# A graph network kernel: slot numbers by one comparing and multiplying operation, lists of 120 edges, the count moved to ScalarE

## The chip, the cores and the metric

The kernel runs on one core of a Trainium2 chip. The core has five engines with queues of their own: TensorE (PE: matrix products, with weight loads shown as PEld), VectorE (DVE), ScalarE (ACT), GpSimd (POOL) and SyncE (SP, which here only issues DMAs). Each engine works through its queue in order and waits on semaphores for the others. The metric is the device time of one execution in microseconds; the median of three runs is what is compared.

## What is computed

The reference takes 6250 nodes with 64 features and 206,250 edges (100,000 drawn pairs in both directions, and a loop at every node), sorted by destination. Cut to what matters:

```python
edge_index = jnp.stack([src, dst])
h = relu(layernorm(x))
# GIN layer, twice: agg = segment_sum(h[src], dst); mlp2(h + agg)
x = x + L0(h, edge_index)
h = relu(layernorm(x))
# message layer: y = mlp3(h[src]); z = segment_sum(y, dst); mlp3([h, z])
x = x + L1(h, edge_index)
```

All three sums over edges use the same 6250 x 6250 matrix of edge counts, A. The kernel builds A from the edge lists once, as one-byte numbers, and then makes matrix products with it.

## The kernel before

**Stages.** Nodes are padded to 49 tiles of 128. From the start to about 375 us the function `fast` builds A tile by tile and takes the first sum over edges from each freshly built tile, with the first layers' products mixed in. Then two sweeps read A back from DRAM for the second and third sum (line 761). A check at the end of the building sets `bad`; where it is set, the slow function `general` computes everything again. It isn't set for these inputs.

**How a tile of A is made.** Two neighbouring destination nodes make a pair, and 128 pairs (one on each partition) make a pair tile; there are 25, one for every two tiles of A. For each pair tile:

- `search` (line 304) and `search_block` (line 328) find where each pair's edges begin, by Sign activations on ScalarE, first over 375 samples and then over a block of 550 gathered destinations.
- `fetch_edges` (line 339) turns that into offsets on VectorE (`off_f`, `off`, lines 344 and 345) and issues one indirect DMA on GpSimd for each pair tile and list: 128 consecutive entries of `dst` into `d_win` and of `src` into `s_win`, for every pair (line 349). `fetch_blocks` (line 319) gathers the blocks for a later batch in the same way (line 324).
- `slots` (line 355) makes three numbers for every entry on VectorE: `word` (which of 32 words), the `high` part of the source (which of 49 columns of tiles), and a `place` number that says which byte of the word and which node of the pair is meant. The windows can hold edges of other pairs. So `mine` (line 376) compares each entry's pair with the partition's own (`which`) and counts the hits in `number`; line 380 then adds -64 to `high` for entries that hit. The one-hot pattern `high2` starts at `HB` = -64, so only those match.
- `cast` (line 392) copies `word` to 16 bits on ScalarE, `turn` (line 396) transposes the three numbers on TensorE, and ScalarE copies them to `lkw` (line 404).
- `hot` (line 406) makes one-hot matrices `there`, `high` and `low` on VectorE, from double-buffered tiles; `build` (line 434) multiplies them for 16 pairs at a time into the PSUM tile `cnt` (line 445; there are two such tiles), and ScalarE evicts each into the tile `a` (line 447). `store` (line 425) sends `a` to DRAM.

**Batches and order.** Pair tiles go in batches of one and then two (`BATCHES`), so that a batch is four tiles of A. The dictionary `beside` (line 523) says between which quarter tiles the steps for later batches are issued: `slots`, `cast` and `turn` one batch ahead, gathers three to four ahead. `follow` and `behind` give the scheduler an order on one engine; otherwise the scheduler places instructions by itself. `FirstSum.quarter` (line 584) puts the first-sum products of the tile before (line 588) between the counts of this one.

**The opening.** Before the rhythm is steady, seven blocks of seven tiles each are normalized (`values`, line 511: `norm` with VectorE steps, a Square and a square root on ScalarE) and each is split into three 16-bit parts (`split`, line 251: products on lines 258 and 260 into `cnt` tiles, copies on lines 255 and 261). Blocks 5 and 6 are issued after tile 0's counts (lines 620 and 624), with `search_block` and `search` for later batches between.

**The check.** `number` has one column per pair tile. Line 652 sums it, lines 656 and 657 count the columns over `SLOTS` = 120, and lines 659 to 668 compare the sums over all partitions with the number of edges, with the summed first-sum counts, and with 0.

Of the kernel before, what the change touches and what calls it, by code (L numbers as in the profile page):

```python
# [32 lines left out]
FP = mybir.dt.float32  # L33
I32 = mybir.dt.int32
I16 = mybir.dt.int16
BF = mybir.dt.bfloat16
# [3 lines left out]
AF = mybir.ActivationFunctionType  # L40
OP = mybir.AluOpType
AX = mybir.AxisListType

P = 128
N = 6250
E = 206250
# [11 lines left out]
H = NT  # L58
G = P // 2
NQ = (NT + 1) // 2  # L60
# [4 lines left out]
BATCHES = (1,) + (2,) * 12  # L65
MOST = max(BATCHES)
SLOTS = 120
# [1 line left out]
W = P // 4  # L69

ONE_BITS, SECOND_BIT, PLACE_BIT = (127 + 2) << 7, 2 + 7, 3 + 7
HB = -64
FIRST_HOTS = ((0, 16), (16, 16), (32, 32))
MIXED = (NT - 8) // 4 + 1
XT = 7
# [83 lines left out]
def fast(ctx: ExitStack, tc: tile.TileContext, x, src, dst, w, bad, out):  # L159

    nc = tc.nc
    dram = ctx.enter_context(tc.tile_pool(name="f_dram", bufs=1, space=bass.MemoryType.DRAM))
    const = ctx.enter_context(tc.tile_pool(name="f_const", bufs=1))
# [10 lines left out]
    def bank(name, dtype=FP):  # L174
        return pmix.tile([P, CH * 4 // mybir.dt.size(dtype)], dtype, tag="mix", name=name)
# [24 lines left out]
    high2 = once.tile([P, H, 2], BF, name="high2")  # L200
    nc.gpsimd.iota(high2, pattern=[[1, H], [0, 2]], base=HB, channel_multiplier=0, allow_small_or_imprecise_dtypes=True)
    which = once.tile([P, NQ], FP, name="which")
    nc.gpsimd.iota(which, pattern=[[P, NQ]], base=0, channel_multiplier=1, allow_small_or_imprecise_dtypes=True)
    ones = const.tile([P, P], FP, name="ones")
    nc.vector.memset(ones, 1.0)
    parts2 = [once.tile([P, MOST, 3, P], BF, name=f"parts{i}") for i in range(2)]


    smp_f = once.tile([SP_ROWS, SP_COLS], FP, name="smp_f")
# [6 lines left out]
    ps = bank("ps_smp")  # L216
# [11 lines left out]
    base = once.tile([P, NQ], FP, name="base")  # L228
    off_f = once.tile([P, NQ], FP, name="off_f")
    off = once.tile([P, NQ], I32, name="off")  # L230
    number = const.tile([P, NQ], FP, name="number")
    sums = const.tile([P, NT], FP, name="sums")

    def norm(to, t, n):
# [42 lines left out]
    wins = building.enter_context(tc.tile_pool(name="f_wins", bufs=2))  # L277
    hots = building.enter_context(tc.tile_pool(name="f_hots", bufs=2))
    starts = [sum(BATCHES[:b]) for b in range(len(BATCHES))]
    blks, lists, lkws = {}, {}, {}  # L280

    def tiles_of(b):
        return range(starts[b], starts[b] + BATCHES[b]), slice(starts[b], starts[b] + BATCHES[b])
# [3 lines left out]
    def behind(op, other):  # L287

        tc.add_manual_dep(op.ins, other.ins.name,
                          mybir.DependencyInfo(mybir.DependencyClass.NoSync, mybir.DependencyReason.DATA),  # L290
                          reason="order on an engine")
        return op

    def follow(op, engine):

        if engine in counted:
            behind(op, counted[engine])
# [30 lines left out]
    def search_block(b, i):  # L328

        if b >= len(BATCHES):  # L330
            return
        q = starts[b] + i
        blk = blks.pop(q)
        junk2 = wins.tile([P, BLK], BF, name="junk2", bufs=1)
        op = nc.scalar.activation(junk2, blk, AF.Sign, bias=below_node[:, q:q + 1], accum_out=sign2[:, q:q + 1])  # L335
        follow(op, "ACT")
        return op

    def fetch_edges(b):

        if b >= len(BATCHES):
            return
        each, qs = tiles_of(b)
        nc.vector.scalar_tensor_tensor(off_f[:, qs], sign2[:, qs], -0.5, base[:, qs], op0=OP.mult, op1=OP.add)
        nc.vector.tensor_scalar(off[:, qs], off_f[:, qs], float(E - P), None, op0=OP.min)  # L345
        lists[b] = [wins.tile([P, MOST, P], I32, name=name)[:, :len(each), :] for name in ("d_win", "s_win")]
        for win, of in zip(lists[b], (dst, src)):
            for i, q in enumerate(each):
                nc.gpsimd.indirect_dma_start(  # L349
                    out=win[:, i, :], out_offset=None, in_=of.rearrange("(a o) -> a o", o=1),  # L350
                    in_offset=bass.IndirectOffsetOnAxis(ap=off[:, q:q + 1], axis=0))

    words = {}

    def slots(b):

        if b >= len(BATCHES):
            return
        each, qs = tiles_of(b)
        n = len(each)  # L360
        d, s = lists.pop(b)

        def temp(name, dtype=I32, tag=None):
            return wins.tile([P, MOST, P], dtype, name=name, tag=tag or name, bufs=1)[:, :n, :]

        parts = parts2[b % 2][:, :n]

        def first(op):
            follow(op, "DVE")

        pair = temp("pair")
        first(nc.vector.tensor_scalar(pair, d, 1, PITCH // 2 - 1, op0=OP.logical_shift_right, op1=OP.bitwise_and))
        pair = pair.bitcast(I16).rearrange("p q (a b) -> p q a b", b=2)
        mine = temp("mine", FP)
        for i, q in enumerate(each):
            nc.vector.tensor_scalar(mine[:, i, :], pair[:, i, :, 0], which[:, q:q + 1], None,
                                    op0=OP.is_equal, op1=OP.add, accum_out=number[:, q:q + 1])
        high = temp("high_i")
        first(nc.vector.tensor_scalar(high, s, 7, 63, op0=OP.logical_shift_right, op1=OP.bitwise_and))
        nc.vector.scalar_tensor_tensor(parts[:, :, 1, :], mine, float(HB), high, op0=OP.mult, op1=OP.add)  # L380
        word = temp("word")
        first(nc.vector.tensor_scalar(word, s, 2, W - 1, op0=OP.logical_shift_right, op1=OP.bitwise_and))
        place = temp("place", tag="high_i")
        first(nc.vector.tensor_scalar(place, s, 3, PLACE_BIT, op0=OP.bitwise_and, op1=OP.logical_shift_left))
        second = temp("second", tag="mine")
        first(nc.vector.tensor_scalar(second, d, 1, SECOND_BIT, op0=OP.bitwise_and, op1=OP.logical_shift_left))
        place, second = (t.bitcast(I16).rearrange("p q (a b) -> p q a b", b=2)[:, :, :, 0] for t in (place, second))
        nc.vector.scalar_tensor_tensor(parts[:, :, 2, :].bitcast(I16), place, ONE_BITS, second,
                                       op0=OP.bitwise_or, op1=OP.bitwise_or)
        words[b] = word  # L390

    def cast(b):
        if b < len(BATCHES):
            follow(nc.scalar.copy(parts2[b % 2][:, :BATCHES[b], 0, :], words.pop(b)), "ACT")

    def turn(b, i):

# [126 lines left out]
    for b in range(len(BATCHES)):  # L524
        step = BATCHES[b]

        def at(u, what, *args):
            beside.setdefault(8 * starts[b] + u * step // 2, []).append((what, args))

        at(0, slots, b + 1)  # L530
        at(4, cast, b + 1)
        for i in range(BATCHES[b + 1] if b + 1 < len(BATCHES) else 0):
            at(7 + 2 * i, turn, b + 1, i)
        if b > 0:
            at(6, search, b + 4)
# [17 lines left out]
    values(0)  # L553
    search_block(0, 0)
    fetch_edges(0)
    values(XT)
    slots(0)
    cast(0)
    for i in range(2):
        op = search_block(1, i)  # L560
    fetch_edges(1)
    turn(0, 0)
    values(2 * XT)
# [84 lines left out]
    hz = late.tile([P, ROWS], FP, name="hz")  # L648


    stats = const.tile([P, 3], FP, name="stats")
    nc.vector.tensor_reduce(stats[:, 0:1], number, axis=AX.X, op=OP.add)
    nc.vector.tensor_reduce(stats[:, 1:2], sums, axis=AX.X, op=OP.add)
    nc.vector.tensor_scalar(stats[:, 1:2], stats[:, 1:2], UNIT, None, op0=OP.mult)
    over = const.tile([P, NQ], FP, name="over")
    nc.vector.tensor_scalar(over, number, float(SLOTS), None, op0=OP.is_gt)
    nc.vector.tensor_reduce(stats[:, 2:3], over, axis=AX.X, op=OP.add)
    ps = bank("ps_stats")
    nc.tensor.matmul(ps[0:1, 0:3], ones[:, 0:1], stats, start=True, stop=True)
    want = const.tile([1, 3], FP, name="want")  # L660
    nc.vector.memset(want[:, 0:1], float(E))
    nc.vector.memset(want[:, 1:2], float(E + ROWS))
    nc.vector.memset(want[:, 2:3], 0.0)
    good = const.tile([1, 3], FP, name="good")
    nc.vector.tensor_tensor(good, ps[0:1, 0:3], want, op=OP.is_equal)
    n_good = const.tile([1, 1], FP, name="n_good")
    nc.vector.tensor_reduce(n_good, good, axis=AX.X, op=OP.add)
    nc.vector.tensor_scalar(bad, n_good, 2.5, None, op0=OP.is_lt)


    follow(nc.vector.tensor_tensor(xs, xs, w.r4[:, None, :].to_broadcast([P, NT, D]), op=OP.add), "DVE")
# [114 lines left out]
    t, n = GROUPS[-1]  # L786
# [257 lines left out]
```

## Time and profile before

| what | value |
|---|---|
| median of three runs | 892.75 us (892.65 to 893.2) |
| the profiled execution | 895.53 us |
| its span, first to last instruction | 893.7 us |
| mean granted TensorE clock | 0.989 |
| TensorE busy | 854.5 us (96%) |
| VectorE busy | 633.7 us (71%) |
| ScalarE busy | 566.0 us (63%) |
| GpSimd busy | 126.9 us (14%) |
| DMA | 148,326 packets, 133.57 MB |

The profile comes from one execution. Busy time is the time in which an engine had an instruction at work; it does not say that the engine set the time. What did is read from the waits: a wait names the engine that the waiting one needed last. In a group's line stand source line, engine, operation, written and read tiles with their shapes, the count, total busy time and mean nanoseconds of one, and then the idle time just before them and who ended it. A timeline's line has the start and the duration first. In a line of a stretch of time, the number after an engine's busy time is its count of instructions, and the last three are the granted TensorE clock, the DMA engines' share and GB/s.

### The profile page before, as it was taken

What the parts mean: (1) busy time and instruction counts of PE and PEld (TensorE: products, weight loads), DVE (VectorE), ACT (ScalarE), POOL (GpSimd) and SP (SyncE); (2) the same over time, 40 slices, a digit from 0 to 9 for tenths busy, and PEclk for the clock granted to TensorE, in tenths of its full rate; (3) what the DMA queues carried; (4) which work ended last, traced back from release to release, by engine and by line L of the source; (5) the groups of instructions that cost most, each with busy time, mean ns of one, the idle gap of its engine ahead of it and who ended that gap; (6) DMA issues with size and microseconds to landing.
All of it is one profiled execution on the core that took longest, in us unless ns stands there. A gap on an engine that the chain in (4) does not pass through costs nothing.

```text
span 893.7 us, 19691 instructions
## 1 busy us (share of the span) xinstructions
PE 854.5 (96%) x8227; PEld 730.8 (82%) x8227; DVE 633.7 (71%) x908; ACT 566.0 (63%) x761; POOL 126.9 (14%) x86
## 2 busy tenths in 40 slices
PE   3789999999999999999999999999999999999996
PEld 1369999999999999978887878888889877777784
DVE  6889999999999999645545555554556676767662
ACT  5757776667776666645555555555546579777763
POOL 4535334354342200000000000000000000000000
PEclk9799999999999999999999999999999999999998
DMA  6335564455545534644444444444434677777771
GB/s 145 103 99 163 150 171 130 140 165 159 142 134 145 148 111 130 198 131 125 129 123 118 124 129 124 118 121 133 128 92 125 181 222 244 232 235 234 218 220 38
DMA packets 148326, 133.57 MB, mean 149 GB/s; under 512 B 29988, under 2 KB 110500, under 8 KB 148228
## 3 DMA queue, kind: packets, MB, share of 16 engines
q1 hardware_dynamic: 141784, 121.19, 46.5%
q0 software_dynamic: 3600, 10.32, 4.4%
q8 instruction: 66, 1.08, 0.5%
q10 hardware_dynamic: 2844, 0.72, 0.4%
q14 instruction: 32, 0.26, 0.1%
HBM read 91.25 MB, written 40.94 MB: 148 GB/s over the span
## 4 chain that ended last, share of the span: by engine, by line
PE 88%; ACT 4%; DMA 3%; DVE 2%; issue 2%; SPq 0%; POOL 0%; ACTq 0%; DVEq 0%
PE acc L761 43%; PE acc L588 23%; PE cnt L445 9%; PE ps_t L458 6%; PE ps_y L467 3%; ACT ar L754 2%; DMA a<-A 2%; PE ps_g L508 1%; PE cnt L258 1%; DMA xs<-in_x_dram 1%; ACT t L460 1%; ACT a L447 1%; PE acc L590 0%; DMA blk<-in_dst_dram,row 0%; PE ps_win L402 0%
## 5 line engine op out<-in xcount | busy, mean ns | idle before, releaser
L754 DVE CAST ar<-a 128x2048 fp32r<-128x2048 uint8 (+1 forms) x200 | 220.4, 1110 | 183.1 <-PE acc L761 158.4
L754 ACT CAST ar<-a 128x2048 fp32r<-128x2048 uint8 (+2 forms) x126 | 232.2, 1845 | 126.4 <-PE acc L761 108.6
L761 PE MATMUL acc<-ar,h2r 128*128 128x512 f32 (+2 forms) x1274 | 297.6, 388 | 0.0
L761 PEld LDWEIGHTS acc<-ar,h2r 128*128 128x128 f32 x1274 | 229.3, 188 | 49.8 <-issue 5.8
L588 PE MATMUL acc<-hp,a 128*128 128x193 bf16 x2401 | 237.1, 247 | 6.6 <-issue 5.8
L447 ACT ACTIVATE a<-cnt 128x784 int16<-128x784 f32 x196 | 160.8, 822 | 83.9 <-PE cnt L445 82.8
L588 PEld LDWEIGHTS <-a 128*128 128x128 fp8e4 x2401 | 196.4, 98 | 10.0 <-issue 7.8
L761 PE MATMUL acc<-ar,yr 128*128 128x512 f32 (+2 forms) x637 | 157.6, 399 | 0.0
L761 PEld LDWEIGHTS acc<-ar,yr 128*128 128x128 f32 x637 | 115.7, 188 | 32.5 <-issue 9.8
L445 PEld LDWEIGHTS <-low 128*128 128x128 fp8e4 x3136 | 107.6, 96 | 10.7 <-issue 10.4
L445 PE MATMUL cnt<-high,low 128*128 128x49 bf16 x3136 | 114.1, 186 | 1.8 <-ACT a L447 1.6
L420 DVE TENSOR_TENSOR low<-there,lkw 128x2048 int32<-128x2048 bf16 (+2 forms) x51 | 112.2, 2199 | 0.0
L417 DVE TENSOR_TENSOR high<-high,lkw 128x3136 bf16<-128x3136 bf16 (+2 forms) x51 | 87.9, 1723 | 19.5 <-PE cnt L445 18.7
L324 POOL DMA_INDIRECT blk<-in_dst_dram,row x25 | 48.0, 1918 | 99.3 <-DVE base L316 86.7
L413 DVE TENSOR_TENSOR there<-word,lkw 128x2048 bf16<-128x2048 bf16 (+2 forms) x51 | 59.1, 1177 | 0.9 <-ACT lkw L404 0.4
L349 POOL DMA_INDIRECT s_win<-in_src_dram,off x25 | 45.4, 1815 | 7.6 <-issue 7.6
L349 POOL DMA_INDIRECT d_win<-in_dst_dram,off x25 | 31.4, 1254 | 72.5 <-DVE off L345 64.9
L258 PE MATMUL cnt<-h,ident 128*128 128x448 f32 x28 | 19.6, 804 | 13.2 <-DVE h L248 9.1
L460 ACT ACTIVATE t<-ps_t,d 128x512 f32<-128x512 f32 (+2 forms) x26 | 17.3, 664 | 11.2 <-PE ps_t L458 11.1
L460 ACT ACTIVATE t<-ps_t,c 128x512 f32<-128x512 f32 (+1 forms) x26 | 17.1, 662 | 11.4 <-PE ps_t L458 11.4
L258 PEld LDWEIGHTS cnt<-h,ident 128*128 128x128 f32 x28 | 5.8, 252 | 19.6 <-issue 10.8
L335 ACT ACTIVATE junk<-blk,below_node 128x550 bf16<-128x550 int32 x25 | 18.7, 749 | 3.8 <-DMA blk<-in_dst_dram,row 3.8
(122 smaller groups left out, 598.2 us busy)
## 6 DMA issues: line engine op xcount, KB each, us to landing
a<-A SPq DMA_DIRECT2D x276, 256.0 KB
A<-a SPq DMA_DIRECT2D x49, 768.0 KB
a<-A SPq DMA_DIRECT2D x24, 192.0 KB
a<-A SPq DMA_DIRECT2D x22, 64.0 KB
out_dram<-o SPq DMA_DIRECT2D x11, 128.0 KB
A<-a SPq DMA_DIRECT2D x49, 16.0 KB
xs<-in_x_dram ACTq DMA_DIRECT2D x3, 224.0 KB
xs<-in_x_dram SPq DMA_DIRECT2D x3, 224.0 KB
```

The lines of the kernel that those rows point to most:

```text
L324: nc.gpsimd.indirect_dma_start(out=blks[q], out_offset=None, in_=dst.rearrange("(r b) -> r b", b=BLK), in_offset=bass.IndirectOffsetOnAxis ...
L349: nc.gpsimd.indirect_dma_start(out=win[:, i, :], out_offset=None, in_=of.rearrange("(a o) -> a o", o=1), in_offset=bass.IndirectOffsetOnAx ...
L413: nc.vector.tensor_tensor(there, word2[:, None, :, :].to_broadcast(shape), of(0)[:, :, None, :].to_broadcast(shape), op=OP.is_equal)
L417: nc.vector.tensor_tensor(high, high2[:, None, :, :].to_broadcast(shape), of(1)[:, :, None, :].to_broadcast(shape), op=OP.is_equal)
L420: counted["DVE"] = nc.vector.tensor_tensor(low.rearrange("p (g i) w -> p g i w", i=2), there.rearrange("p g w i -> p g i w"), of(2)[:, :, ...
L445: counted["PE"] = nc.tensor.matmul(ps[:, b, j * H:(j + 1) * H], low[:, g, :], high[:, g // 2, :, g % 2], start=True, stop=True)
L447: counted["ACT"] = nc.scalar.activation(a[:, :, k:k + 2 * PG].rearrange("p h (b j) -> p h b j", b=2), ps[:, :, :PG * H].rearrange("p b (j ...
L458: placed(nc.tensor.matmul(ps[:, :n * P], wt, rhs, start=(i == 0), stop=(i == len(terms) - 1)))
L460: nc.scalar.activation(to, ps[:, :n * P], AF.Relu, bias=bias)
L588: nc.tensor.matmul(acc[:, t % 2, :], self.a[:, k, :], hp[:, k], start=(k == 0), stop=False)
L754: widen(ar.rearrange(f"p k t b -> {order}"), a.rearrange(f"p t (k b) -> {order}", b=P))
L761: op = nc.tensor.matmul(acc[:, :n * P], part, ar[:, k - k0].rearrange("p t b -> p (t b)"), start=(k == 0 and i == 0), stop=(k == H - 1 and ...
```

## The change

The lists that are gathered become 120 long instead of 128, and all tiles of `slots` with them; the last 8 of the 128 slots of `parts` are set to zero once by GpSimd. `HB` becomes +64: `high` gets bit 6 set by an or in the same tensor_scalar that shifts it. One `scalar_tensor_tensor` for each pair tile then compares the pair with `which` and multiplies the result with `high`, straight into `parts`: an own entry becomes 64 + its column, any other 0, which no column of `high2` matches. `mine`, its count and the adding of `HB` go away. `place` and `second` get tiles of their own instead of sharing.

The count is made by ScalarE in `cast`: a Sign of the `high` numbers less 32 gives +1 for an own entry and -1 for another, summed over a batch into one column of `number`. The sum to be met changes accordingly, and the count of columns over 120 goes away, since a list can't hold more.

```diff
-HB = -64
+HB = 64
+assert H <= HB
...
+    for t in parts2:
+        nc.gpsimd.memset(t[:, :, :, SLOTS:], 0.0)
...
-    number = const.tile([P, NQ], FP, name="number")
+    number = const.tile([P, len(BATCHES)], FP, name="number")
+    between_hb = const.tile([P, 1], FP, name="between_hb")
+    nc.vector.memset(between_hb, -HB / 2)
...
-        nc.vector.tensor_scalar(off[:, qs], off_f[:, qs], float(E - P), None, op0=OP.min)
-        lists[b] = [wins.tile([P, MOST, P], I32, name=name)[:, :len(each), :] for name in ("d_win", "s_win")]
+        nc.vector.tensor_scalar(off[:, qs], off_f[:, qs], float(E - SLOTS), None, op0=OP.min)
+        lists[b] = [wins.tile([P, MOST, SLOTS], I32, name=name)[:, :len(each), :] for name in ("d_win", "s_win")]
...
-        parts = parts2[b % 2][:, :n]
+        parts = parts2[b % 2][:, :n, :, :SLOTS]
...
-        mine = temp("mine", FP)
+        high = temp("high_i")
+        first(nc.vector.tensor_scalar(high, s, 7, HB, op0=OP.logical_shift_right, op1=OP.bitwise_or))
         for i, q in enumerate(each):
-            nc.vector.tensor_scalar(mine[:, i, :], pair[:, i, :, 0], which[:, q:q + 1], None,
-                                    op0=OP.is_equal, op1=OP.add, accum_out=number[:, q:q + 1])
-        high = temp("high_i")
-        first(nc.vector.tensor_scalar(high, s, 7, 63, op0=OP.logical_shift_right, op1=OP.bitwise_and))
-        nc.vector.scalar_tensor_tensor(parts[:, :, 1, :], mine, float(HB), high, op0=OP.mult, op1=OP.add)
+            nc.vector.scalar_tensor_tensor(parts[:, i, 1, :], pair[:, i, :, 0], which[:, q:q + 1], high[:, i, :],
+                                           op0=OP.is_equal, op1=OP.mult)
...
-        place = temp("place", tag="high_i")
+        place = temp("place")
...
-        second = temp("second", tag="mine")
+        second = temp("second")
...
-            follow(nc.scalar.copy(parts2[b % 2][:, :BATCHES[b], 0, :], words.pop(b)), "ACT")
+            parts = parts2[b % 2][:, :BATCHES[b], :, :SLOTS]
+            follow(nc.scalar.copy(parts[:, :, 0, :], words.pop(b)), "ACT")
+            junk = wins.tile([P, MOST, SLOTS], BF, name="junk3", bufs=1)[:, :BATCHES[b], :]
+            follow(nc.scalar.activation(junk, parts[:, :, 1, :], AF.Sign, bias=between_hb, accum_out=number[:, b:b + 1]), "ACT")
...
-    over = const.tile([P, NQ], FP, name="over")
-    nc.vector.tensor_scalar(over, number, float(SLOTS), None, op0=OP.is_gt)
-    nc.vector.tensor_reduce(stats[:, 2:3], over, axis=AX.X, op=OP.add)
...
-    nc.vector.memset(want[:, 0:1], float(E))
+    nc.vector.memset(want[:, 0:1], float(E - (NQ * P * SLOTS - E)))
...
-    nc.vector.memset(want[:, 2:3], 0.0)
...
-    nc.vector.tensor_scalar(bad, n_good, 2.5, None, op0=OP.is_lt)
+    nc.vector.tensor_scalar(bad, n_good, 1.5, None, op0=OP.is_lt)
```

More of the change, by code (lines that the diff above doesn't have):

```diff
@@ L363, in temp @@
         def temp(name, dtype=I32, tag=None):
-            return wins.tile([P, MOST, P], dtype, name=name, tag=tag or name, bufs=1)[:, :n, :]
-        parts = parts2[b % 2][:, :n]
+            return wins.tile([P, MOST, SLOTS], dtype, name=name, tag=tag or name, bufs=1)[:, :n, :]
+        parts = parts2[b % 2][:, :n, :, :SLOTS]
         def first(op):
@@ L648, in fast @@
     hz = late.tile([P, ROWS], FP, name="hz")
-    stats = const.tile([P, 3], FP, name="stats")
+    stats = const.tile([P, 2], FP, name="stats")
     nc.vector.tensor_reduce(stats[:, 0:1], number, axis=AX.X, op=OP.add)
@@ L654, in fast @@
     nc.vector.tensor_scalar(stats[:, 1:2], stats[:, 1:2], UNIT, None, op0=OP.mult)
-    over = const.tile([P, NQ], FP, name="over")
-    nc.vector.tensor_scalar(over, number, float(SLOTS), None, op0=OP.is_gt)
-    nc.vector.tensor_reduce(stats[:, 2:3], over, axis=AX.X, op=OP.add)
     ps = bank("ps_stats")
-    nc.tensor.matmul(ps[0:1, 0:3], ones[:, 0:1], stats, start=True, stop=True)
-    want = const.tile([1, 3], FP, name="want")
-    nc.vector.memset(want[:, 0:1], float(E))
+    nc.tensor.matmul(ps[0:1, 0:2], ones[:, 0:1], stats, start=True, stop=True)
+    want = const.tile([1, 2], FP, name="want")
+    nc.vector.memset(want[:, 0:1], float(E - (NQ * P * SLOTS - E)))
     nc.vector.memset(want[:, 1:2], float(E + ROWS))
-    nc.vector.memset(want[:, 2:3], 0.0)
-    good = const.tile([1, 3], FP, name="good")
-    nc.vector.tensor_tensor(good, ps[0:1, 0:3], want, op=OP.is_equal)
+    good = const.tile([1, 2], FP, name="good")
+    nc.vector.tensor_tensor(good, ps[0:1, 0:2], want, op=OP.is_equal)
     n_good = const.tile([1, 1], FP, name="n_good")
     nc.vector.tensor_reduce(n_good, good, axis=AX.X, op=OP.add)
-    nc.vector.tensor_scalar(bad, n_good, 2.5, None, op0=OP.is_lt)
+    nc.vector.tensor_scalar(bad, n_good, 1.5, None, op0=OP.is_lt)
     follow(nc.vector.tensor_tensor(xs, xs, w.r4[:, None, :].to_broadcast([P, NT, D]), op=OP.add), "DVE")
```

## The prediction

> **What bounds the kernel now.** The page's slices come first: they tell which engine is full in which stretch.
>
> ```profile
> ## 2 busy tenths in 40 slices
> PE   3789999999999999999999999999999999999996
> ...
> DVE  6889999999999999645545555554556676767662
> ...
> PEclk9799999999999999999999999999999999999998
> ```
>
> The change touches the first 16 slices (0 to about 375 us, building and first sum). There TensorE and VectorE both read 9, so the slices can't say which holds the other. Stretches of my own choice and the waits from 60 to 375 us can:
>
> ```profile
> core 0: us, PE busy (x) PEld busy (x) DVE busy (x) ACT busy (x) POOL busy (x), PEclk, DMA share, GB/s
> 0.00:60.00 60.00, 37.36 (x259) 20.08 (x260) 45.16 (x123) 36.67 (x86) 28.63 (x34) 0.89 0.44 109
> 60.00:318.00 258.00, 251.97 (x4510) 244.49 (x4509) 239.59 (x294) 179.61 (x311) 98.29 (x52) 1.00 0.53 148
> 318.00:375.00 57.00, 57.00 (x1033) 55.64 (x1031) 48.47 (x48) 35.42 (x53) 0.00 (x0) 1.00 0.50 147
> ```
>
> ```profile
> PE acc L588 <- issue: 5.8, 9, 0.7
> ```
>
> ```profile
> DVE high L417 <- PE cnt L445: 18.4, 12, 2.0
> ```
>
> From 60 us on TensorE is idle for 6.0 us in all, in nine gaps of 0.65 us; in none is VectorE named. VectorE does wait for TensorE, 12 times: `high` may not overwrite a buffer that the counts still read. So **TensorE bounds this stage**, and VectorE is up to 2.0 us ahead in each batch of four tiles (27.58 us between the starts of L458 at 174.40 and 201.97). The chain agrees: 88% PE, 2% DVE. After 375 us nothing that the change edits runs, except the small sums of `stats`. What is left is the opening, where TensorE works 37 of 60 us, and the nine gaps. One gap in the timeline:
>
> ```profile
> 188.62 0.82 ACT L447 ACTIVATE a<-cnt 128x784 int16<-128x784 f32 x1 [0.61 <-PE cnt L445]
> ...
> 189.21 0.94 POOL L349 DMA_INDIRECT d_win<-in_dst_dram,off  x1 [4.34 <-DVE off L345]
> ...
> 189.45 0.57 PE L445 MATMUL cnt<-high,low 128*128 128x49 bf16 x16
> ...
> 190.12 1.22 DVE L413 TENSOR_TENSOR there<-word,lkw 128x2048 bf16<-128x2048 bf16 x1
> ...
> 190.46 1.70 POOL L349 DMA_INDIRECT d_win<-in_dst_dram,off  x1 [0.30 <-issue]
> ...
> 191.31 1.79 ACT L447 ACTIVATE a<-cnt 128x784 int16<-128x784 f32 x2 [1.81 <-PE cnt L445]
> ...
> 192.19 1.28 PE L588 MATMUL acc<-hp,a 128*128 128x193 bf16 x13 [0.64 <-issue]
> ```
>
> The counts started at 189.45 are done at 190.02, yet their eviction starts at 191.31, and the next first-sum products wait for it. The named releaser was long done. The gap comes in each of the nine batches (84.5 to 302.3 us) in which GpSimd issues window gathers there; in the next two batches VectorE does the same slot work without gathers, and the eviction at 327.54 is not late. So I tie the gap to the gathers, which stay. Its mechanism I can't name.
>
> **The change, part by part.** VectorE, a batch of two pair tiles. The rows, of 0 to 345 us:
>
> ```profile
> L376 DVE TENSOR_SCALAR_CACHE_REDUCE mine<-pair,which 128x128 f32<-128x128 int16 x25 | 7.6, 340 | 0.1
> ...
> L380 DVE SCALAR_TENSOR_TENSOR parts<-mine,high_i 128x256 bf16<-128x256 f32 x12 | 5.0, 417 | 0.0
> ...
> L376 DVE DVE_READ_ACCUMULATOR mine<-pair,which 128x1 f32 x25 | 2.0, 82 | 0.0
> ```
>
> Out go 2 x (340 + 82) + 417 = 1261 ns. In come two comparing and multiplying operations over 120 elements. The nearest row is L380's single form, 277 ns for 128; at (417 - 277)/128 = 1.1 ns an element that is 268 ns, so 536 ns. Shrinking 256 to 240 saves 16 x 0.6 ns on five tensor_scalars (48 ns) and 18 ns on L388. Busy time saved: about 0.79 us a batch, 9.9 us over 12.5 batches. **On the path from 60 us: nothing.** In 188.5 to 192 us the slots end earlier, then `high` waits for TensorE, 2.0 us becoming 2.8. That cover would have to be gone before any of it counted.
>
> ScalarE, a batch: the cast shrinks from 397 to about 385 ns, and one Sign over 240 with its accumulator read follows it. Nearest rows: L311, 616 ns for 375, and L335, 749 ns for 550, hence 0.76 ns an element and 513 ns for 240; its read (195 ns) overlaps, so the queue moves by 0.5 us. Behind it stands the second eviction of a tile (at 200.98, after 0.36 us of idleness): 0.15 us late. TensorE needs that bank two units later (after a unit and 1.5 us of L458, with 0.70 us more idleness on ScalarE), and the transposes wait for the cast alone. Cost: nothing; without that slack 0.15 to 0.5 us a batch, at most 6 us.
>
> GpSimd: two memsets of 128x48 before the first gather, which waits 7.57 us for `row`; and one block gather of batch 4 moves ahead of the window gathers of batch 3, which are then some 1.3 us later (its row near 10 us) and needed tens of us on. Nothing. `stats`: two operations of 168 ns and a memset fewer, beside TensorE's full stretch. Nothing.
>
> Gathers: packets of 480 instead of 512 bytes, 6400 of them. The Trainium skill (DMA: Bandwidth & Descriptors, Specifications) says that under 512 bytes a transfer falls below line rate because of read-modify-write; that speaks against the lists of 120. The row: in the chain the first `s_win` takes 3.48 us from issue to landing for 64 KB, which at the mean 99 GB/s of 10 to 60 us is 0.7 us of moving, the rest latency. By the row the change is -0.04 us, by the rule up to +0.5 (an estimate: the moving part not quite doubled) for each gather on the path, and only two in the opening are; later ones are fetched three batches (80 us) ahead. I take +0.2, ends 0 and +1.
>
> The new operation reads two tensors, the old one a single tensor with an accumulator. The skill (SBUF — State Buffer, Who interferes with whom) says that a VectorE operation with two SBUF inputs locks out a GpSimd read. The row agrees in kind: the `d_win` gather takes 0.94 us beside the old comparisons and 1.70 beside `there`. By the rule the first one may now take 1.70 too; by the row as it stands it stays 0.94. GpSimd idles 4.34 us before it, so the sum is nothing either way, 0 to +0.5 in the opening.
>
> **The opening** is where the order moves: the scheduler places the shorter slots differently, and the built order of the changed kernel shows this. (1) The root for value block 4 now precedes two block searches that wait for gathers until 29.88 and 31.49, so its `h` comes about 0.8 us sooner; the new Sign (0.5) before tile 0's last eviction eats most of that. (2) Blocks 5 and 6, formerly split apart, are now split back to back, after 35 first-sum products. Before, block 6 starts its split at 51.23, and the steady rhythm starts at 59.56. Now, from tile 0's last eviction (end 41.6, as before): ScalarE 0.36 lkw + 0.46 square + 2 x 0.75 + 2 x 0.72 searches = 45.4; VectorE 0.2 + 1.14 (`there`) + 0.12 + 0.53 + 0.62 = 48.0; TensorE splits block 5 in 1.56 + 0.37 + 1.3 + 0.55 = 3.8, so block 6 starts at 51.8, 0.6 late. (3) The clock: at 52 to 54 us it is 0.50 after the idle 49.0 to 51.2, so block 6's products are slow (1.56 us against 1.02 at 28.61). Now the slow ones are block 5's and block 6 runs warm, about -0.8. Together -0.2, with ends -2 and +3, since the gate's phase and each wait are guesses.
>
> **Sum:** steady part 0, opening -0.2 + 0.2 = 0.0 on the profiled execution's 895.53 (span 893.7, 1.8 around it). The median of the runs, 892.75, moves by the same: **892.8 us**, no change.
>
> **Rivals.** *Faster: the nine gaps go.* They end 0.05 us after `there`, as if VectorE's slot sequence held them; the shift of order there (`place` and `second` now ahead of `there`) may free the eviction. Then 9 x 0.65 = 5.9: 886.9; half of it 889.8. Against: `there` stays 1.5 us after L344 (1.6 now), and the gathers stay. An opening better by 2 lands at 890.8. *Slower: the opening.* The two splits in a row become the bound: if block 5's `h` comes after about 49 us and the clock drops again before block 6, +0.6, +1.7 (half of 3.4 us of split at half clock) and +0.8 of gathers give +3.1: 895.9. It decides from 1.8 us on. For it: every link is in a queue with four searches ahead. *It does not do what it says*: the counting moves out of VectorE, surely, but to an engine with slack from one with slack; that is the forecast itself.
>
> **How the numbers follow.** Forecast 0.46, faster cases 0.26 (gaps 0.14, opening 0.12), slower 0.28. A measurement can tell 0.2%, 1.8 us, so 891.0 to 894.5 is "same". The range 888.5 to 896.0 holds the forecast and most of both sides; left out are the gaps gone in full and an opening worse by over 3. The likeliest case alone: 891.0 to 894.5.
>
> **What would show it.** Right: VectorE's busy time down by 9 to 10 us, its wait for TensorE in `high` up by about as much, nine gaps of 0.65, ScalarE's busy time up by 6 to 8, and block 6's split at 51 to 52.5. Wrong: gaps of another size or number; an eviction wait at the Sign that TensorE feels; the first steady tile more than 2 us away from 59.6; or a slower sweep after 375 us, which nothing here would explain.

## The result, and the profile after

| | before | after |
|---|---|---|
| median | 892.7 us (892.58 to 893.2, 6 runs) | 899.58 us (896.47 to 901.54, 6 runs) |
| the profiled execution, its span | 895.53, 893.7 us | 900.75, 898.9 us |
| GpSimd busy | 126.9 us | 154.1 us |
| VectorE busy | 633.7 us | 628.6 us |
| ScalarE busy | 566.0 us | 568.9 us |

The change made the kernel **slower**: the ratio is 1.0073, 95% interval 1.0058 to 1.0089, or 6.9 us between the medians. The range of the prediction ended at 896.0.

The slices of the page after, from the same part as those shown of before:

```profile
## 2 busy tenths in 40 slices
PE   3699999999999999999999999999999999999996
...
DVE  5899998898888989654454555545555786767662
```

VectorE's nines have become eights, which looks like the saving that was planned. TensorE's row tells nothing: a 9 hides up to a tenth. The stretches show it:

```profile
60.00:318.00 258.00, 246.00 (x4380) 237.82 (x4378) 229.38 (x262) 176.64 (x324) 120.10 (x52) 1.00 0.51 144
318.00:375.00 57.00, 57.00 (x1011) 55.01 (x1009) 51.04 (x44) 36.80 (x58) 0.00 (x0) 1.00 0.47 132
```

TensorE is busy for 246.00 us of 258 where it was 251.97: its idle time has doubled from 6.0 to 12.0 us, all of it in the stretch in which GpSimd works too. From 318 us on, where no gathers are left, it is full as before. The waits of that stretch (engine and line, whom it waited for, total us, times, longest):

```profile
ACT a L453 <- PE acc L596: 15.3, 7, 2.2
...
PE acc L594 <- ACT a L453: 10.4, 16, 0.7
...
PE cnt L451 <- issue: 1.4, 7, 0.2
```

Nine gaps have become sixteen. Nine stand where they stood (for instance at 192.99, beside `there`), and in seven batches there is a **second gap** 8.2 us later. In each of these seven TensorE also stops for 0.2 us just before the gap (at 200.26, for instance), between two counts, in a wait for which the profile names nobody; that is the last line above. The seven batches take 28.75 us from layer product to layer product (174.99 to 203.73, for instance) instead of 27.58: 7 x 1.17 = 8.2 us. The first such start is 91.70 in place of 93.18, so the opening gave back 1.5. Together +6.7 at the last of these starts (371.7 against 365.0). From there to the end the changed execution is 1.5 us the shorter, which leaves 5.2 us between the two profiled executions; the medians are 6.9 us apart.

The groups that grew or came, from the list of groups of after (count, busy us, mean ns, idle before):

```profile
L354 POOL DMA_INDIRECT d_win<-in_dst_dram,off x25 | 72.4, 2897 | 61.5 <-DVE high_i L380 53.4 <-issue 3.7 <-DVE off L350 3.0
...
L382 DVE SCALAR_TENSOR_TENSOR parts<-pair,which,high_i 128x120 bf16<-128x120 int16 x25 | 7.5, 337 | 0.0
L400 ACT ACTIVATE junk<-parts,between_hb 128x240 bf16<-128x240 bf16 (+1 forms) x13 | 6.4, 494 | 0.0
```

A `d_win` gather took 1254 ns on average before and takes 2897 now. The mean mixes two kinds; the timeline of one second gap separates them:

```profile
191.43 5.75 POOL L354 DMA_INDIRECT d_win<-in_dst_dram,off  x1 [0.30 <-issue]
194.08 2.29 DVE L426 TENSOR_TENSOR low<-there,lkw 128x2048 int32<-128x2048 bf16 x1
...
196.40 1.22 DVE L419 TENSOR_TENSOR there<-word,lkw 128x2048 bf16<-128x2048 bf16 x1
...
197.48 0.96 POOL L354 DMA_INDIRECT s_win<-in_src_dram,off  x1 [0.30 <-issue]
...
198.11 0.58 PE L451 MATMUL cnt<-high,low 128*128 128x49 bf16 x16
...
198.75 0.94 POOL L354 DMA_INDIRECT s_win<-in_src_dram,off  x1 [0.30 <-issue]
...
200.35 1.54 ACT L453 ACTIVATE a<-cnt 128x784 int16<-128x784 f32 x2 [2.17 <-PE acc L596]
200.35 1.79 DVE L423 TENSOR_TENSOR high<-high,lkw 128x3136 bf16<-128x3136 bf16 x1 [1.11 <-PE acc L596]
...
201.23 1.28 PE L594 MATMUL acc<-hp,a 128*128 128x193 bf16 x13 [0.64 <-ACT a L453]
```

Read it from below. TensorE's products at 201.23 need the eviction that starts at 200.35. That evicts the counts of 198.11, the last of a tile, which are done at 198.69. So the eviction starts 1.66 us after them; VectorE's `high`, which waits for the same counts, starts in the same moment. It is thus **TensorE's signal that comes late**, not one engine that dawdles. And around it stand two `s_win` gathers, which before were issued at 192.46 and 194.57, in the middle of a tile. They come at the tile end now since the second `d_win` gather, 1.70 us long before, lasts from 191.43 to 197.18.

### The profile page after: what moved, and what is told of

Same layout as the page of the kernel before. It is cut to its first block, busy times and chain, and to the rows that moved or that the text cites. A ratio compares the mean times of both kernels' runs of the same rounds, so it can differ in the third digit from the quotient of the medians.

```text
span 898.9 us, 19681 instructions
## 1 busy us (share of the span) xinstructions
PE 854.5 (95%) x8227; PEld 731.0 (81%) x8227; DVE 628.6 (70%) x868; ACT 568.9 (63%) x787; POOL 154.1 (17%) x88
## 2 busy tenths in 40 slices
DMA packets 148326, 133.36 MB, mean 148 GB/s; under 512 B 29988, under 2 KB 110500, under 8 KB 148228
## 4 chain that ended last, share of the span: by engine, by line
PE 85%; ACT 6%; DMA 4%; DVE 3%; issue 2%; SPq 0%; POOL 0%; ACTq 0%; DVEq 0%
PE acc L763 41%; PE acc L594 21%; PE cnt L451 10%; PE ps_t L464 5%; PE ps_y L473 3%; DMA a<-A 3%; ACT ar L756 2%; ACT a L453 2%; PE ps_g L514 1%; DVE ar L756 1%; PE cnt L263 1%; PE acc L596 1%; ACT t L466 1%; DMA xs<-in_x_dram 1%; DMA blk<-in_dst_dram,row 0%
## 5 line engine op out<-in xcount | busy, mean ns | idle before, releaser
L451 PEld LDWEIGHTS <-low 128*128 128x128 fp8e4 x3136 | 107.2, 96 | 11.6 <-issue 11.1
L354 POOL DMA_INDIRECT d_win<-in_dst_dram,off x25 | 72.4, 2897 | 61.5 <-DVE high_i L380 53.4
L329 POOL DMA_INDIRECT blk<-in_dst_dram,row x25 | 50.2, 2008 | 90.7 <-DVE base L321 70.9
L354 POOL DMA_INDIRECT s_win<-in_src_dram,off x25 | 29.1, 1166 | 7.6 <-issue 7.6
L263 PE MATMUL cnt<-h,ident 128*128 128x448 f32 x28 | 17.5, 729 | 11.9 <-DVE h L253 6.4
L466 ACT ACTIVATE t<-ps_t,d 128x512 f32<-128x512 f32 (+2 forms) x26 | 17.3, 664 | 11.2 <-PE ps_t L464 11.1
```

The lines of the kernel that those rows point to most:

```text
L329: nc.gpsimd.indirect_dma_start(out=blks[q], out_offset=None, in_=dst.rearrange("(r b) -> r b", b=BLK), in_offset=bass.IndirectOffsetOnAxis ...
L354: nc.gpsimd.indirect_dma_start(out=win[:, i, :], out_offset=None, in_=of.rearrange("(a o) -> a o", o=1), in_offset=bass.IndirectOffsetOnAx ...
L451: counted["PE"] = nc.tensor.matmul(ps[:, b, j * H:(j + 1) * H], low[:, g, :], high[:, g // 2, :, g % 2], start=True, stop=True)
L466: nc.scalar.activation(to, ps[:, :n * P], AF.Relu, bias=bias)
```

## The experiments

### One part undone at a time, and the same kernels on other chips

Four kernels ran on one chip, each 22 times, beside 75 runs of the kernel before.

`place` and `second` behind `there` again, by buffers that they share as before:

```diff
-        place = temp("place")
+        place = temp("place", tag="high_i")
-        second = temp("second")
+        second = temp("second", tag="pair")
```

> The changed kernel with one thing undone: place and second share buffers with high_i and pair again, so that VectorE runs them behind the comparison there, as the old kernel does. Theory (order): with place and second ahead of there, GpSimd's second d_win gather is caught by the big VectorE operations that follow and takes 5.75 us; s_win's gathers come later by that and spoil a second tile end. Then here that gather is back near 1.7 us, the seven second gaps of 0.68 us are gone, and the time is 899.6 minus about 8 = 891 to 892 us. Rival (the new comparing operation, the 480-byte lists or the Sign do it): the gather stays at 5.75 us, the gaps stay, 899 to 900 us.

The old kernel with lists of 120 alone:

```diff
-        nc.vector.tensor_scalar(off[:, qs], off_f[:, qs], float(E - P), None, op0=OP.min)
-        lists[b] = [wins.tile([P, MOST, P], I32, name=name)[:, :len(each), :] for name in ("d_win", "s_win")]
+        nc.vector.tensor_scalar(off[:, qs], off_f[:, qs], float(E - SLOTS), None, op0=OP.min)
+        lists[b] = [wins.tile([P, MOST, SLOTS], I32, name=name)[:, :len(each), :] for name in ("d_win", "s_win")]
...
```

> The old kernel with lists of 120 edges alone (and the unused 8 columns set to zero once); it compares, counts and orders as before. Theory (order): 892 to 893.5 us, nine gaps of 0.65 us, second d_win gather near 1.7 us. Rival (480-byte packets slow the gathers): second gaps appear, the second d_win gather is several us long, 898 to 900 us.

The changed kernel without the Sign:

```diff
-            follow(nc.scalar.activation(junk, parts[:, :, 1, :], AF.Sign, bias=between_hb, accum_out=number[:, b:b + 1]), "ACT")
```

> The changed kernel without the Sign on ScalarE: the count of own edges is left out, and the last test asks for one of its two sums. Theory (order): the second gaps and the 5.75 us gather stay, 899 to 900 us. Rival (the Sign delays an eviction): the second gaps go, 891 to 893 us.

The gathers half a batch later:

```diff
+        if b > 1:
+            at(5, fetch_edges, b + 2)
...
-            at(13, fetch_edges, b + 3)
```

> The changed kernel with the window gathers fetched some 6 us later: two batches ahead instead of three, VectorE's second offset operation behind low instead of between the slot operations. Theory (a tile end is spoiled when a window gather runs across it): the gaps move with the gathers. Their number changes (each batch has none, one or two of 0.65 us), so 884 to 900 us; at 83.0, 108.8, 135.5 us and so on nothing is left. Rival (the slot operations themselves hold the eviction): the first gaps stay where they are, beside there.

All four missed, in the same way: 882.26, 882.21, 882.10 and 881.55 us, beside a kernel before at **883.51** instead of 892.7. In none does TensorE have a gap of the kind from 60 to 318 us. In the first the second `d_win` gather took 5.93 us and not 1.7, with the old order; the last part of the experiments comes back to that. So nothing was told apart, but something was learned: the gaps are not in the program alone. The unchanged pair on yet another chip:

> The changed kernel itself, once more, since the four runs before it showed no gap at all from 60 to 318 us, with the old kernel at 883.5 us beside them. Theory (the gaps belong to the chip or its condition, not to the program): where the old kernel takes 883 to 884 us, this one has no gaps either and takes 881 to 883 us, like the others; where the old one takes 892 to 893 us, this one takes 897 to 901 us with sixteen gaps. Rival (the changed order makes gaps anywhere): sixteen gaps and about 9 us more than the old kernel on any chip.

> The old kernel unchanged, for its profile beside the changed one's on the same chip. Theory (the gaps belong to the chip): at 883 to 884 us no gap from 60 to 318 us, at 892 to 893 us nine gaps of 0.65 us. Rival (the program makes them): nine gaps on any chip.

882.72 us for the changed kernel, 883.27 for the old one; ratio of the changed one 0.9986, 0.9976 to 0.9996. The stretch from 60 to 318 us of the changed kernel there, and then of the old one:

```profile
60.00:318.00 258.00, 257.77 (x4659) 251.37 (x4657) 242.19 (x277) 186.81 (x338) 120.11 (x52) 1.00 0.54 151
```

```profile
60.00:318.00 258.00, 257.80 (x4658) 251.31 (x4657) 246.88 (x307) 182.94 (x318) 98.30 (x52) 1.00 0.54 152
```

Neither has a gap. GpSimd's times are those of the first chip, 120 and 98 us, down to the long gather. The place of the second gap, on this chip:

```profile
182.51 5.75 POOL L354 DMA_INDIRECT d_win<-in_dst_dram,off  x1 [0.31 <-issue]
...
188.39 0.58 PE L451 MATMUL cnt<-high,low 128*128 128x49 bf16 x16
188.57 0.96 POOL L354 DMA_INDIRECT s_win<-in_src_dram,off  x1 [0.30 <-issue]
...
189.00 0.82 ACT L453 ACTIVATE a<-cnt 128x784 int16<-128x784 f32 x1 [0.55 <-PE cnt L451]
```

The same long gather, an `s_win` gather beside the tile's last counts, and the eviction starts 0.03 us after they end. Two things are needed for a gap: a chip on which TensorE's signal comes late beside a window gather, and such a gather placed so that the late signal is that of a tile's last counts. The first is a property of the chip (or its state; each chip was met once); the program decides only the second.

Not every gather of GpSimd does it, even on the first chip. There, in the kernel before, a block gather runs while the last counts of a tile end, at 184.09:

```profile
182.91 1.96 POOL L324 DMA_INDIRECT blk<-in_dst_dram,row  x1 [0.30 <-ACT lkw L404]
...
183.52 0.57 PE L445 MATMUL cnt<-high,low 128*128 128x49 bf16 x16
...
184.16 0.81 ACT L447 ACTIVATE a<-cnt 128x784 int16<-128x784 f32 x1
```

The eviction follows at once. Of all counts that end under one of the 16 block gathers from 60 to 318 us, none waits more than 0.22 us for its eviction. So the late signal goes with the window gathers; what sets these apart wasn't tested.

### One kernel with batches of several kinds

Since the gaps depend on the chip, the next kernel carries its comparison in itself.

```diff
+    OLD, DIRECT, MOVED = (4, 7), (5, 8), (6, 9)
...
+                if b - 3 in DIRECT:
+                    nc.sync.dma_start(win[:, i, :], of[q % 8 * P * SLOTS:(q % 8 + 1) * P * SLOTS].rearrange("(p c) -> p c", p=P))
+                    continue
...
+        place = temp("place", tag="high_i" if b - 1 in OLD else None)
+        second = temp("second", tag="pair" if b - 1 in OLD else None)
...
+            if b not in MOVED:
+                at(13, fetch_edges, b + 3)
+            if b - 1 in MOVED:
+                at(5, fetch_edges, b + 2)
```

> The changed kernel with its batches treated in different ways, so that one profile compares them: batches 1 to 3 as they are; in 4 and 7 VectorE runs place and second behind there, as in the old kernel; in 5 and 8 the window gathers are replaced by plain loads of as many bytes through SP (part of the computation left out: those batches get other edges, and the last test is not asked); in 6 and 9 the gathers come half a batch later. Where the chip shows no gaps (the old kernel at 883 us) nothing is told apart: 26.8 us between the starts of the layer products in every batch, whatever the treatment. Where it shows them (892 us): theory (a tile end is spoiled where GpSimd writes out a window gather): control two gaps of 0.65 us, old order one, plain loads none, moved ones at another place. Rival (the data that lands does it, whoever issued it): plain loads have the gap too. Rival (VectorE's slot operations do it): plain loads and moved gathers leave the first gap beside there.

It met a chip with gaps (kernel before: 894.1 us; this one 890.61). The slot operations of turn 4 are executed beside the gathers of turn 3, so the old order stands in the batch that ends at 143.69; that of turn 7 stands beside no gather. TensorE's gaps and layer products, in order of time:

```profile
116.20 0.71 PE L469 MATMUL ps_t<-f,w1p 128*128 128x512 f32 x2
134.14 1.28 PE L602 MATMUL acc<-hp,a 128*128 128x193 bf16 x13 [0.57 <-issue]
143.69 0.71 PE L469 MATMUL ps_t<-f,w1p 128*128 128x512 f32 x2
161.68 1.28 PE L602 MATMUL acc<-hp,a 128*128 128x193 bf16 x13 [0.62 <-ACT a L458]
...
169.90 1.28 PE L602 MATMUL acc<-hp,a 128*128 128x193 bf16 x13 [0.66 <-ACT a L458]
172.41 0.71 PE L469 MATMUL ps_t<-f,w1p 128*128 128x512 f32 x2
199.16 0.71 PE L469 MATMUL ps_t<-f,w1p 128*128 128x512 f32 x2
225.91 0.71 PE L469 MATMUL ps_t<-f,w1p 128*128 128x512 f32 x2
```

Old order: one gap, 27.49 us. As changed: two gaps, 28.72 us. Window gathers replaced by plain loads: none, 26.75 us. Gathers half a batch later: none, 26.75 us. A second batch as changed (28.71 us) and a second one with plain loads (26.75 us) say the same. So VectorE's slots don't make a gap, since they run unchanged in the batches without gathers (188.35 for `there`): the window gathers do, and only where the late signal is that of a tile's last counts. With the moved gathers an eviction is late too, 0.66 us at 224.24, but it is that of a tile's first counts, which TensorE needs only a tile later.

The rival "the data that lands does it" is not settled by the plain loads. SyncE issued those for turn 5 from 159.54 to 161.38, a batch early; at the tile ends of turn 5 no window data landed at all. What speaks against it is the kernel before: from 190.02, where the counts of the prediction's gap end, to 190.86 the DMA engines stand still (share 0.00), and the data of the gather move only from 190.86 to 191.37, when the signal is 0.8 us late already.

The second such kernel asks which gather makes which gap:

```diff
-    OLD, DIRECT, MOVED = (4, 7), (5, 8), (6, 9)
+    OLD, DIRECT, MOVED = (7,), (), ()
...
-                if b - 3 in DIRECT:
+                if b - 3 in ((4, 7) if of is src else (5, 8)):
```

> The changed kernel with its batches treated in different ways a second time: in 4 and 7 only d_win is gathered and s_win comes by plain loads through SP, in 5 and 8 only s_win is gathered and d_win comes by plain loads (part of the computation left out: those batches get other edges, and the last test is not asked); in 6 the two operations place and second stand behind there, in 1 to 3 and 9 nothing is changed. On a chip without gaps: nothing is told apart, 26.8 us from batch to batch. On a chip with gaps: theory (the second gap comes from the s_win gathers, which the long d_win gather pushes onto the next tile end): d_win alone one gap a batch, s_win alone one (it then stands where d_win stood), batch 6 one, unchanged batches two. Rival (the 5.75 us gather itself spoils both tile ends): d_win alone keeps two gaps.

A chip with gaps again (before 896.69, this 895.85):

```profile
117.33 0.71 PE L469 MATMUL ps_t<-f,w1p 128*128 128x512 f32 x2
135.36 1.28 PE L602 MATMUL acc<-hp,a 128*128 128x193 bf16 x13 [0.67 <-ACT a L458]
...
143.58 1.28 PE L602 MATMUL acc<-hp,a 128*128 128x193 bf16 x13 [0.67 <-ACT a L458]
146.09 0.71 PE L469 MATMUL ps_t<-f,w1p 128*128 128x512 f32 x2
164.09 1.29 PE L602 MATMUL acc<-hp,a 128*128 128x193 bf16 x13 [0.63 <-ACT a L458]
173.65 0.71 PE L469 MATMUL ps_t<-f,w1p 128*128 128x512 f32 x2
191.65 1.28 PE L602 MATMUL acc<-hp,a 128*128 128x193 bf16 x13 [0.64 <-ACT a L458]
201.21 0.71 PE L469 MATMUL ps_t<-f,w1p 128*128 128x512 f32 x2
219.21 1.28 PE L602 MATMUL acc<-hp,a 128*128 128x193 bf16 x13 [0.64 <-issue]
228.77 0.71 PE L469 MATMUL ps_t<-f,w1p 128*128 128x512 f32 x2
```

As changed two gaps (28.76 us); `d_win` alone one, `s_win` alone one, the old order one, each batch 27.56 us. The `d_win` gather alone still takes 5.75 us and yet makes no second gap: the second is that of the `s_win` gathers behind it, as the theory had it. A first gap costs 27.56 - 26.75 = 0.81 us, a second one 1.2.

### Whole kernels again

The old order and the moved gathers were run as whole kernels four more times, to meet a chip with gaps; the edits are those of the first section.

> The changed kernel with all window gathers moved half a batch later (as in e4_a_mid5), for its time on a chip with gaps. Theory (TensorE's signal is late while GpSimd has a window gather under way, and that costs only where it is the last count of a tile): no gaps, since the gathers now fall between two tile ends; where the old kernel takes 892 to 894 us, this one takes 884 to 888 us; where the old one takes 883 us, 881 to 883 us, as before. Rival (gathers cost 0.65 us wherever they stand): 892 us or more on a chip with gaps.

> The changed kernel with place and second behind there again (as in e1_tags), for its time on a chip with gaps. Theory (their order makes the second gap): nine gaps of 0.6 us in place of sixteen; where the old kernel takes 892 to 894 us, this one is within 2 us of it, so 7 us faster than the change as it is. Rival (the Sign, the new operation or the lists of 120 make the second gap): sixteen gaps, some 7 us slower than the old kernel.

> The changed kernel with all window gathers half a batch later, once more, one look, in the hope of a chip with gaps. Theory (a window gather costs only where TensorE's late signal is the one of a tile's last count): no gap from 60 to 318 us on any chip; beside an old kernel at 892 to 894 us it takes 884 to 888 us. Rival (it costs wherever it stands): nine gaps or more on such a chip.

> The changed kernel with place and second behind there, once more, one look, in the hope of a chip with gaps. Theory (their order makes the second gap): nine gaps on such a chip and 890 to 893 us; none and 881 to 883 us on the others. Rival: sixteen gaps, 897 to 901 us.

> The changed kernel with all window gathers half a batch later, for its time on a chip with gaps (chips 0 and 9 had them, 2, 10, 12 and 14 not). Theory (a gather costs only at a tile end): no gap; beside an old kernel at 892 to 897 us it is 5 to 9 us faster than that; beside one at 883 us it is 1 to 2 us faster. Rival (it costs wherever it stands): as slow as the old kernel or slower on a chip with gaps.

> The changed kernel with place and second behind there in every batch. Theory (the second gap is the whole loss): beside an old kernel at 892 to 897 us, nine gaps and a time within 2 us of it; beside one at 883 us, 1 to 2 us less. Rival (part of the loss has another cause): slower than the old kernel by more than 2 us on a chip with gaps.

Three chips without gaps, so these missed their aim: 881.63, 882.17 and 882.73 us for the moved gathers, 882.20, 882.46 and 882.54 for the old order, beside a kernel before at 883.95, 881.43 and 885.3.

> The changed kernel with all window gathers half a batch later, one look on another chip. Theory: no gap on any chip; beside an old kernel at 892 to 897 us, 5 to 9 us faster than that; beside one at 881 to 885 us the same within 3 us. Rival (a gather costs wherever it stands): nine gaps or more beside an old kernel at 892 us or more.

> The changed kernel with place and second behind there in every batch, one look on another chip. Theory: nine gaps beside an old kernel at 892 to 897 us, and a time within 3 us of it; none beside one at 881 to 885 us. Rival (part of the loss has another cause): more than nine gaps, or over 3 us slower than the old kernel.

This chip had the gaps; one run of each: before 892.7, the old order **892.66**, the moved gathers **887.8**. The waits of TensorE from 60 to 318 us, for the old order and then for the moved gathers:

```profile
PE acc L594 <- issue: 5.7, 9, 0.7
```

```profile
PE acc L595 <- ACT a L453: 1.4, 5, 0.3
```

Nine gaps, as before the change, and its time. So, as far as one run of each shows, the order of two short operations is the whole loss; the changed kernel itself was not run on this chip. The moved gathers have five gaps of 0.3 us left, where none was expected, and are 4.9 us faster than the kernel before. They still run across tile ends:

```profile
191.25 1.73 POOL L354 DMA_INDIRECT d_win<-in_dst_dram,off  x1 [11.23 <-DVE off L350]
...
192.53 0.82 ACT L453 ACTIVATE a<-cnt 128x784 int16<-128x784 f32 x1 [0.55 <-PE cnt L451]
```

The counts evicted at 192.53 are a tile's last, and they are done at 192.50. The late signal, 1.4 us in seven batches, is now that of the next tile's first counts (done at 194.02, evicted at 195.43). The five gaps are what comes of it: ScalarE is behind by then and is still at a search when a tile's last counts are done, so it evicts them 1.1 us later (200.89 for 199.77). On the four chips without gaps this version is level with the other variants; where it ran often enough for an interval its ratio to before is 0.9985 (0.9974 to 0.9995), 0.9979 (0.9965 to 0.9994) and 0.9967 (0.9955 to 0.9978). It is the version to keep.

### Why the order matters to a gather

On this chip, in the old order:

```profile
188.57 1.71 POOL L354 DMA_INDIRECT d_win<-in_dst_dram,off  x1 [0.30 <-issue]
...
189.19 0.27 DVE L389 TENSOR_SCALAR second<-d_win 128x240 int32<-128x240 int32 x1
189.45 1.79 ACT L453 ACTIVATE a<-cnt 128x784 int16<-128x784 f32 x2 [1.83 <-PE cnt L451]
189.45 1.79 DVE L423 TENSOR_TENSOR high<-high,lkw 128x3136 bf16<-128x3136 bf16 x1
```

And the same kernel on a chip without gaps:

```profile
182.09 5.93 POOL L354 DMA_INDIRECT d_win<-in_dst_dram,off  x1 [0.30 <-issue]
...
182.70 0.28 DVE L389 TENSOR_SCALAR second<-d_win 128x240 int32<-128x240 int32 x1
182.89 1.78 DVE L423 TENSOR_TENSOR high<-high,lkw 128x3136 bf16<-128x3136 bf16 x1
...
184.92 2.28 DVE L426 TENSOR_TENSOR low<-there,lkw 128x2048 int32<-128x2048 bf16 x1
187.23 1.22 DVE L419 TENSOR_TENSOR there<-word,lkw 128x2048 bf16<-128x2048 bf16 x1
```

By these times the gather gets through where VectorE pauses, and ends 0.82 us later. In the second fence each operation follows the last without a pause until `low` ends at 187.20 and `there` starts at 187.23; the gather ends at 188.02. In the changed kernel on the first chip: `low` ends at 196.37, `there` starts at 196.40, the gather ends at 197.18. In the first fence `high` starts 0.26 us after `second`, not 0.19, in the moment in which the late signal releases ScalarE; the gather ends at 190.28, 0.83 us after that. So, as it seems, in the old order VectorE stands at `high` for the very signal that makes the first gap, and this lets the gather in. In the changed order line 391 follows `there` at once, `high` comes 0.4 us later (192.38) and finds the signal there, and no pause comes for two more operations. What fits less well is the kernel before: there the gather ends 0.82 us after `there` (191.34), though `place` overlaps it by 0.08. Which handovers let a gather in isn't settled.

## Why the prediction was wrong, step by step

- **TensorE bounds this stage, VectorE's saving is worth nothing there.** Right. VectorE's busy time fell by 5.1 us (5.4 on the chip of the unchanged pair), not by 9 to 10: the new operation takes 337 ns, not 268, which is 25 x 69 = 1.7 us; by the rows 8.2 us are gone, and the total, which counts overlapping instructions once, shows less: the 82 ns reads of the accumulator, which the forecast took as saved, had run under the next operation. On that chip `high` waits 5.1 us longer for TensorE (16.2 against 11.1 from 60 to 375 us): the saving went into that wait, as forecast.
- **ScalarE's Sign is hidden.** Right on every chip: no gap stands behind it, and in the mosaic kernels it runs in batches with no gap. It takes 494 ns; 513 were worked out. ScalarE's busy time rose by 2.9 us, and by 5.2 on the chip of the unchanged pair, not by 6 to 8.
- **The opening, 0.0 in all.** Right in its links: block 6 is split at 51.40 (51.8 was worked out). The 1.5 us that it gained on the first chip were not forecast; they lie beside a granted clock of 0.94 up to 60 us instead of 0.89, and block 5's first products, expected to be slow, took 0.99 us (block 6's 0.91, and 1.56 before); on the chip of the unchanged pair, with 0.97 for both, the first layer product starts at 87.56 against 87.50.
- **Packets of 480 bytes, +0.2.** Nothing to be seen: the old kernel with lists of 120 has 0.9986 (0.9976 to 0.9996), like the changed one. All variants with short lists have ratios of 0.9967 to 0.9986 on the chips without gaps, where they ran 20 times or more, which points to a small gain of the lists; it was not isolated further. Nor is the rule that the prediction cited tested: the profile records no packets of 480 bytes for a gather but 16 of 3840 (4096 before), and its page counts 29,988 packets under 512 bytes before and after.
- **The step that failed**: "the gathers stay", and with it the price of the port that VectorE and GpSimd share, "nothing either way, 0 to +0.5 in the opening". The rule of the Trainium skill (SBUF — State Buffer, Who interferes with whom) was cited rightly in kind: a gather is held while VectorE's two-input operations run. But its term was sized by one operation, 0.94 or 1.70 us, and looked up in the opening alone. The first gather of a batch, for which it was asked, came out at 1.12 us. The second one, which already stood beside `there` for 1.70 us, now takes 5.75 us in each of the nine batches: the rule gives the lock for one instruction, and here the gather was held through a run of four (`there`, line 391, `high`, `low`). That by itself is hidden, as forecast: with `d_win` alone the 5.75 us make no second gap. What it pushes isn't: two `s_win` gathers onto a tile end, 1.17 us in each of seven batches, 8.2 us.
- **Rivals.** The nine gaps were tied to the gathers, which was right (batches without window gathers: none), but the rival "the gaps go" took the move of `place` and `second` for a chance to free the eviction, which was said to start 0.05 us after `there` (it starts 0.03 us before `there` ends, 191.31 against 191.34). The same move did the opposite. No rival had the gaps become more.
- **What would show it wrong** named "gaps of another size or number", and that is what came.

## What to carry to other kernels

Where an engine off the path feeds transfers, ask where in the consumer's rhythm they fall: here a late signal cost TensorE 0.65 us where it was a tile's last, and little or nothing where it was the first. Before reordering short VectorE operations, look for the pause in which GpSimd gets its gather out: here a run of operations without one delayed all gathers behind it. And measure on more than one chip before believing a 1% difference: here it was +0.7% on one and -0.1% on another, with the same program.

## What was not expected of the hardware

- The same program has TensorE's signals 1.2 to 1.7 us late beside window gathers on some chips (0, 7, 9 and that of the first comparison) and not at all on others (2, 6, 10, 12, 14). The kernel before takes 892 to 897 us on the ones and 881 to 885 us on the others. The gaps aren't all of that difference: its first layer product starts at 93.18 us on the first chip, one gap included, and at 87.50 us on chip 10, beside a granted clock of 0.89 and 0.97 up to 60 us. What differs between the chips isn't known, nor by which way a window gather holds up a signal of TensorE, nor why a block gather doesn't. The skill page named above has TensorE and ScalarE wait for nobody at the SBUF ports, and the traces agree in so far as TensorE's own products run on meanwhile, but for the 0.2 us stops before the second gaps.
- A gather that takes 0.94 us beside other operations took 4.8 us more beside a run of VectorE operations, and ended 0.81 us after a pause of 0.03 us between two of them.
